# First layernorm of a transformer block: token-major rows and on-chip transposes replaced by embedding-major loads, with means and deviations applied separately

## The chip, the cores and the metric

The kernel runs on one core of a Trainium2 chip. The core has five instruction streams: TensorE (PE, matrix products, with its weight loads shown as PEld), VectorE (DVE), ScalarE (ACT), GpSimd (POOL) and SyncE (SP), which here issues every DMA. Each stream is executed in the order written, so an instruction that waits holds all behind it on its engine. The metric is the time of one execution in microseconds, median of several; all data are float32.

## The reference, cut to what matters

```python
def _layernorm(x, axis=-1, eps=1e-05):
    m = jnp.mean(x, axis=axis, keepdims=True)
    v = jnp.var(x, axis=axis, keepdims=True)
    return (x - m) / jnp.sqrt(v + eps)
...
    q = (hidden_states @ Wq).reshape(b, s, HEADS, HEAD_DIM)
    k = (hidden_states @ Wk).reshape(b, s, HEADS, HEAD_DIM)
    v = (hidden_states @ Wv).reshape(b, s, HEADS, HEAD_DIM)
    q, k = rotary(q), rotary(k)
    logits = jnp.where(causal, einsum('bhqd,bhkd->bhqk', q, k), MASK_VAL) / sqrt(64)
    out = einsum('bhqk,bhkd->bhqd', softmax(logits), v)
    return out.reshape(b, s, e) @ Wo
...
    x = x + _layernorm(attention(_layernorm(x)))
    x = x + _layernorm(ffn(_layernorm(x)))
```

There are 8 sequences (batches) of 512 tokens, an embedding of 1024, 16 heads of 64. The feed-forward part is one 1024x1024 product with a bias and a low-rank adapter. The change concerns the innermost layernorm, the one ahead of Wq, Wk and Wv. The mean and the deviation are one number per token, so (x - m)/d times a weight equals ((x - m) times the weight)/d. For q and k, d can therefore also be put into the cosine and sine tables of the rotary step, since these are multiplied onto every element of a token.

## The kernel before

All large products use two levels of Strassen-Winograd: 49 products of blocks in place of 64. The kernel goes through four stages: values (V = layernorm(x) @ Wv, batch after batch, and in passing the operands of x for later), q and k with attention, Wo, and the feed-forward part. The change touches the first stage, and the tables of the second.

**The V stage.** A loop over 8 batches, each of 7 groups of 7 products: 49 ticks (`N2`) a batch. In one tick PE does one 128x256 product over 256 rows (two calls, L315, four instructions in the trace). A group's products go into four accumulators: a and d with one buffer, b and c with two. The order in a group is P6 (accumulator b), P1 (a), P3 of the group before (c), P5 (c), P4 (d), P7 (b again), P2 (a again). They are drained one tick later (`Group.drain`, L334): P1 by a copy on ACT and the sum `u2 = p1 + b` on DVE, P7 by three sums on DVE, P2 by a copy on ACT, P3 by a sum on DVE. P7 accumulates onto the buffer that `u2` reads. Results are put together in tiles `c11`, `c21`, `c12`, `c22`, `U`, `A` (`COMBINE`, L358, some on DVE, some on POOL) and stored to `vd` by `store_v`.

**What is written by hand.** Nothing is planned by a scheduler: `at(tick, fn)` puts a function into a list, and `run` writes out, tick after tick, first what is marked "pe", then the tick's product with the drain of the one before, then the rest in order of registration. The order of instructions on each engine, SP too, is the order of these ticks.

**Operands of x.** While batch b is multiplied, `plan_x(b + 1, base)` (L468) prepares the next, with base = 49 b:
- ticks base-12 to base-9: four loads of 128 tokens x 1024 (`load_x`).
- ticks base+4 to base+23: mean and variance of each row (`stats`, L390: two `bn_stats`, an aggregate, a root on ACT, a reciprocal, a bias), and the norm on ACT in two halves (L415).
- ticks base+11, 18, 25, 32 and the ticks after each: four transposes each on PE (L449) and a copy on ACT into a tile of the right operand, `R11`, `R21`, `R12`, `R22` (L457).
- three ticks after the first transposes: the four differences of a tile on POOL (`sub_right`, L263).
- ticks 38, 45, 52, 63: the sums of tiles T1 (DVE), T2, T4 (POOL), T3 (DVE) (`sum_right`, L275). Tiles of one batch take the buffers of the batch before, by `next_roles`; T2 takes the buffer of the batch's T2, which product 44 is the last to read.
- each finished tile is also stored to `xop` for the second stage (`store_operand`, L463, 0.92 MB each).

**Weight sums.** In batches 1 to 7 the sums of one eighth of the q and k weights of the first half of the heads are made (`plan_part`, `plan_sums` L547, name `g0`): load at base (L553), eight operations on POOL at base+4 to base+11 (L562), store at base+16 (L565, 1568 KB in pieces of 256 bytes). The last batch does a second eighth on DVE.

**Second stage.** `plan_unit` (L691) forms q and k for two batches and half of the heads in a unit of 49 ticks, loads weights and operands of each tick 8 ticks ahead into a ring (`load_slot`, L606), and `rotate` (L660) multiplies by tables `cos` and `sin` (one of 128x512 each for all batches, loaded in `start_attention`). The attention of the unit before runs in between.

Of the kernel before, what the change touches and what calls it, by code (L numbers as in the profile page):

```python
# [132 lines left out]
def sandwich_kernel(  # L133
    ctx: ExitStack,
    tc: tile.TileContext,
    x: bass.AP,
    wqk: bass.AP,
# [31 lines left out]

    vd = [dram.tile([P, NT, E], F32, name=f"vd_{b}") for b in range(B)]  # L170
# [258 lines left out]
    xp = early.enter_context(tc.tile_pool(name="xp", bufs=4))  # L429
    chp = early.enter_context(tc.tile_pool(name="ch0", bufs=2))  # L430
    xs = {}
    dve, pool = nc.vector, nc.gpsimd

    def load_x(b, t):
        xs[b, t] = xp.tile([P, E], F32, tag="x", name=f"x_{b}_{t}")
        nc.sync.dma_start(out=xs[b, t], in_=x[b, ts(t, P), :])

    def stats_x(b, t, step):
        stats(f"v{b}_{t}", [xs[b, t][:, ts(h, HALF)] for h in range(2)], step)

    def norm_x(b, t):
        for h in range(2):
            v = xs[b, t][:, ts(h, HALF)]
            norm(f"v{b}_{t}", v, v)

    def transpose_x(b, t, g):
        pt = ps_t.tile([P, NH, P], F32, tag="tp", name=f"ptx_{b}_{t}_{g}")
        for k in range(NH):
            nc.tensor.transpose(pt[:, k, :], xs[b, t][:, ts(NH * g + k, P)], ident)  # L449
        return pt  # L450

    def keep_x(b, t, g, pt):
        h, c = divmod(t, 2)
        n = f"R{g + 1}{h + 1}"
        if c == 0:
            open_right(gvp, b - B, n)
        nc.scalar.copy(  # L457
            RX[b - B, n][:, 2 * c : 2 * c + 2], pt[:, :, :].rearrange("p (k c) n -> p k c n", k=2)
        )
# [4 lines left out]

    def store_v(b, tag, half, h):
        nc.sync.dma_start(out=vd[b][:, 2 * h : 2 * h + 2, ts(half, HALF)], in_=C[b - B, tag])

    def plan_x(b, base):  # L468

        at(base + 10, next_roles)  # L470
        for t in range(NT):
            at(max(0, base - 12) + t, lambda t=t: load_x(b, t))
            k = (4, 5, 17, 19)[t]
            for m in range(4):
                at(base + k + m, lambda t=t, m=m: stats_x(b, t, m))
            at(base + k + 4, lambda t=t: norm_x(b, t))
        for n, k in (("R11", 11), ("R21", 18), ("R12", 25), ("R22", 32)):
            g, h = int(n[1]) - 1, int(n[2]) - 1
            for c in range(2):
                t = 2 * h + c  # L480
                at(base + k + c, lambda t=t, g=g: transpose_x(b, t, g), "pe")
                at(base + k + c, lambda pt, t=t, g=g: keep_x(b, t, g, pt), "post")
            at(base + k + 3, lambda n=n: sub_right(b - B, n, pool))
# [7 lines left out]
        for n, k in (  # L491
            ("R11", 18), ("R21", 25), ("R22", 40), ("T1", 44), ("T2", 54), ("T4", 60), ("T3", 69)
        ):
            at(base + k, lambda n=n: store_operand(b, n))

    def prepare(t):
        for m in range(4):
            stats_x(0, t, m)
        norm_x(0, t)

    tags = {"L11": "L11", "L12": "L12", "L22": "L22", "L21": "S3"}
    nc.scalar.activation(eps_sd, eps, AF.Sqrt)
    for n in (0, 1, "L11", 2, 3, "L12", "L22", "L21"):
        if isinstance(n, int):
            load_x(0, n)
        else:
            load_left(wvp if n == "L21" else wvl, wv, n, tags[n])
    for t in range(2):
        prepare(t)
    for g in range(2):  # L510
        for t in range(2):
            keep_x(0, t, g, transpose_x(0, t, g))
    for k in range(4):
        sub_left("L11", k, dve)
# [3 lines left out]
    sub_right(-B, "R11", dve)  # L518
    at(0, lambda: sub_right(-B, "R21", dve))
    for t in (2, 3):  # L520
        at(t - 2, lambda t=t: prepare(t))
    for g in range(2):
        for t in (2, 3):
            at(3 + 2 * g + t - 2, lambda t=t, g=g: transpose_x(0, t, g), "pe")
# [836 lines left out]
```

## Time and profile before

| | us |
|---|---|
| runs before (3) | 2499.87, 2498.07, 2499.29; median 2499.29 |
| span of the profiled execution | 2491.9 |
| PE busy in the span | 2394.2 (96%) |
| DVE, POOL, ACT busy | 1744.9, 1490.5, 1094.4 |
| V stage: first product to first product of stage two | 13.0 to 431.8 |
| transposes L449 in it (x256), PE busy | 43.7 |
| bn_stats L395 (x64), norms L415 (x64) | 41.9, 48.6 |
| weight sums L562 on POOL to 420 us (x56) | 64.5 |
| DMA: q1 share of 16 engines over the span | 73.9% |

The span is 7.4 us shorter than the median of the runs, which also hold what lies before the first and after the last instruction. Rows of a timeline give the start, the length, the engine, the line, output and inputs, and in brackets the idle time of the engine before it and what ended that. Busy times of matmuls overlap, since they are pipelined; the distance between starts tells more. In names, a number such as -5 is the batch minus 8 (so -5 is batch 3), and the number after it only tells buffers apart.

### The profile page before, as it was taken

What the parts mean: (1) busy time and instruction counts of PE and PEld (TensorE: products, weight loads), DVE (VectorE), ACT (ScalarE), POOL (GpSimd) and SP (SyncE); (2) the same over time, 40 slices, a digit from 0 to 9 for tenths busy, and PEclk for the clock granted to TensorE, in tenths of its full rate; (3) what the DMA queues carried; (4) which work ended last, traced back from release to release, by engine and by line L of the source; (5) the groups of instructions that cost most, each with busy time, mean ns of one, the idle gap of its engine ahead of it and who ended that gap; (6) DMA issues with size and microseconds to landing.
All of it is one profiled execution on the core that took longest, in us unless ns stands there. A gap on an engine that the chain in (4) does not pass through costs nothing. (4 is left out here: it accounts for less than half of the span.)

```text
span 2491.9 us, 37087 instructions
## 1 busy us (share of the span) xinstructions
PE 2394.2 (96%) x12192; PEld 1880.4 (75%) x12192; DVE 1744.9 (70%) x3849; ACT 1094.4 (44%) x2749; POOL 1490.5 (60%) x1119
## 2 busy tenths in 40 slices
PE   6999999999999999999999999899999999999997
PEld 4787887877677777777777776458888878888886
DVE  8777767475857759486775957766777777766676
ACT  3323331026555556555555565763444544222222
POOL 3878875215263454637465363426777687888885
PEclk8999999999999999999999999899999999999999
DMA  7697787999899898988989895657566676434334
GB/s 261 198 299 251 241 272 235 344 307 285 238 302 285 258 328 255 328 267 297 326 264 346 250 327 174 219 182 266 178 202 212 217 278 240 137 126 153 132 106 140
DMA packets 415665, 606.00 MB, mean 243 GB/s; under 512 B 127889, under 2 KB 243601, under 8 KB 410866
## 3 DMA queue, kind: packets, MB, share of 16 engines
q1 hardware_dynamic: 415474, 603.64, 73.9%
q8 instruction: 98, 1.61, 0.3%
q14 instruction: 93, 0.76, 0.1%
HBM read 368.65 MB, written 201.33 MB: 229 GB/s over the span
## 5 line engine op out<-in xcount | busy, mean ns | idle before, releaser
L778 ACT ACTIVATE pr<-pr,nm 128x128 f32<-128x128 f32 (+3 forms) x512 | 280.9, 550 | 169.7 <-DVE nm L768 169.6
L792 ACT ACTIVATE pr<-pr,rs 128x128 f32<-128x128 f32 (+2 forms) x500 | 245.2, 549 | 119.9 <-DVE rs L786 119.8
L768 DVE CUSTOM_DVE_ANT_0 pr<-s,mask 128x128 f32<-128x128 f32 (+3 forms) x512 | 224.1, 484 | 41.8 <-PE s L747 39.7
L636 PE MATMUL acca_q_P<-xs,ls 128*128 128x256 f32 x896 | 217.3, 385 | 0.8 <-issue 0.8
L636 PE MATMUL accc_q_P<-xs,ls 128*128 128x256 f32 x896 | 217.7, 386 | 0.0
L636 PE MATMUL accb_q_P<-xs,ls 128*128 128x256 f32 x896 | 216.3, 384 | 0.8 <-DVE u_q_P L116 0.8
L1107 POOL TENSOR_TENSOR c<-c,row 128x512 f32<-128x512 f32 x120 | 160.7, 1360 | 87.4 <-ACT c L415 80.3
L636 PEld LDWEIGHTS acca_q_P<-xs,ls 128*128 128x128 f32 x896 | 165.3, 190 | 49.9 <-issue 19.1
L636 PEld LDWEIGHTS accc_q_P<-xs,ls 128*128 128x128 f32 x896 | 165.8, 190 | 48.4 <-issue 23.2
L636 PEld LDWEIGHTS accb_q_P<-xs,ls 128*128 128x128 f32 x896 | 165.4, 190 | 44.9 <-issue 6.2
L275 POOL TENSOR_TENSOR T<-R,T 128x512 f32<-128x512 f32 (+1 forms) x96 | 174.1, 1840 | 41.4 <-DVE u_P L337 21.0
L747 PE MATMUL s<-qk 64*128 64x128 f32 (+3 forms) x1024 | 193.8, 474 | 5.1 <-DVE nm L768 4.7
L806 PE MATMUL ptp<-ident,pr 128*128 128x128 f32 x1280 | 178.7, 278 | 11.0 <-DVE nm L768 4.8
L806 PEld LDWEIGHTS ptp<-ident,pr 128*128 128x128 f32 x1280 | 147.7, 142 | 43.1 <-ACT pr L792 15.8
L827 PE MATMUL po<-pT,v 128*64 128x512 f32 (+3 forms) x1024 | 157.4, 446 | 9.7 <-ACT pT L821 9.7
L562 POOL TENSOR_TENSOR wc_g<-wc_g 128x256 f32<-128x256 f32 (+1 forms) x120 | 124.1, 1053 | 65.5 <-DMA wc_g<-in_wqk_dram 43.5
L678 POOL TENSOR_TENSOR B_q<-B_q,m 128x1024 f32<-128x1024 f32 x14 | 35.0, 2497 | 199.0 <-DVE B_q L675 199.0
L827 PEld LDWEIGHTS po<-pT,v 128*64 128x64 f32 x1024 | 72.4, 139 | 102.0 <-issue 66.5
L337 DVE TENSOR_TENSOR p_P<-accb_P,p_P 128x256 f32<-128x256 f32 x109 | 45.0, 413 | 102.4 <-PE accb_P L315 53.5
L636 PE MATMUL accd_q_P<-xs,ls 128*128 128x256 f32 x448 | 108.7, 385 | 0.0
L337 DVE TENSOR_TENSOR u_P<-accb_P,p_P 128x256 f32<-128x256 f32 x109 | 46.1, 423 | 89.1 <-ACT p_P L342 89.0
L747 PEld LDWEIGHTS s<-qk 64*128 64x128 f32 x1024 | 73.1, 187 | 46.2 <-issue 27.9
(1108 smaller groups left out, 5809.7 us busy)
## 6 DMA issues: line engine op xcount, KB each, us to landing
ls<-wqk SPq DMA_DIRECT2D x392, 256.0 KB, 4.9
xs<-xop SPq DMA_DIRECT2D x392, 256.0 KB, 5.2
R<-attn SPq DMA_DIRECT2D x32, 896.0 KB, 5.5
wqk<-wc_g SPq DMA_DIRECT2D x16, 1568.0 KB, 9.3
x<-in_x_dram SPq DMA_DIRECT2D x32, 512.0 KB, 9.5
v<-vd SPq DMA_DIRECT2D x64, 256.0 KB, 5.0
attn<-ops SPq DMA_DIRECT2D x16, 1024.0 KB, 7.8
row<-in_x_dram SPq DMA_DIRECT2D x32, 512.0 KB, 5.9
```

The lines of the kernel that those rows point to most:

```text
L275: eng.tensor_tensor(RX[q, n][:, c], RX[q, x][:, c], RX[q, y][:, c], op=ALU.subtract)
L337: add = lambda out, x, a: nc.vector.tensor_tensor(out, acc[a], x, op=ALU.add)
L562: eng.tensor_tensor(out, x, y, op=op)
L636: nc.tensor.matmul(acc[:, :, w, :], lhsT=ls[:, k, w, :], rhs=xs_[:, :, k, :], start=(first and w == 0 and k == 0), stop=True, skip_group_c ...
L678: eng.tensor_tensor(v, v, m[step - 4, q], op=ALU.add)
L747: nc.tensor.matmul(ps[:, j, at : at + L], lhsT=qT[r, qb], rhs=kT[r, : qb + 1], start=True, stop=True,)
L768: nc.vector.tensor_tensor_reduce(out=v[:, j, :], in0=self.ps[qb][:, j, :], in1=work2["mask"][:, S - L :], scale=-1.0 / HD**0.5, scalar=3.0e38,
L778: nc.scalar.activation(v[:, j, :], v[:, j, :], AF.Exp, bias=nm[:, j : j + 1], scale=-1.0, accum_out=sm[:, j : j + 1],)
L792: nc.scalar.mul(v, v, rs[:, j : j + 1])
L806: nc.tensor.transpose(pt[:, n, :], self.pr[qb][:, j, ts(kb, P)], ident)
L827: nc.tensor.matmul(po[j * HD : (j + 1) * HD, kb * P :], lhsT=self.v[:, kb, ts(j, HD)], rhs=self.pT[j][:, kb, kb * P :], start=(kb == 0), s ...
L1107: nc.gpsimd.tensor_tensor(c, c, row[q, t][:, ts(h, HALF)], op=ALU.add)
```

## The change

The embedding-major form of x is a second input, `xt`, laid out on the host like the tiles `R11` to `R22`. Each tile is loaded straight into its operand buffer. The rows are still loaded, as one transfer of 2 MB a batch, only for sums and squared deviations, on ACT. The negative means go through a small DRAM tile `std` and come back spread over all partitions; `center` adds them to a loaded tile on DVE. For batch 0 the means are made on PE by products with a matrix of -1/1024. The operands are then centred but not divided. The inverse deviation goes onto the finished values (`scale_v`, ACT, ahead of each `store_v`) and, again by `std`, onto tables `tab0` and `tab1` of each unit of stage two (`load_inverse`, `scale_trig` on POOL), which `rotate` uses in place of `cos` and `sin`. The differences of the tiles move one tick or so later, and stores of tiles and values by up to three.

```diff
+    std = [dram.tile([2, S], F32, name=f"std_{b}") for b in range(B)]
...
-    xp = early.enter_context(tc.tile_pool(name="xp", bufs=4))
+    xp = early.enter_context(tc.tile_pool(name="xp", bufs=1))
+    mean_w = xp.tile([P, P], F32, name="mean_w")
+    nc.gpsimd.memset(mean_w, -1.0 / E)
...
+    def load_rows(b):
+        xs[b] = xp.tile([P, NT, E], F32, tag="x", name=f"x_{b}")
+        nc.sync.dma_start(out=xs[b], in_=x[b].rearrange("(t p) e -> p t e", p=P))
+        moments[b] = env["small"].tile([P, 4, NT], F32, tag="mom", name=f"mom_{b}")
+    def sum_rows(b, t):
+        m = moments[b]
+        nc.scalar.activation(xs[b][:, t], xs[b][:, t], AF.Copy, accum_out=m[:, 0, t : t + 1])
+    def square_rows(b, t):
+        m = moments[b]
+        nc.scalar.activation(
+            xs[b][:, t], xs[b][:, t], AF.Square, bias=m[:, 1, t : t + 1], scale=1.0,
+            accum_out=m[:, 2, t : t + 1],
+        )
...
+    def store_moment(b, w):
+        nc.sync.dma_start(
+            out=std[b][w].rearrange("(t p) -> p t", p=P), in_=moments[b][:, 1 + 2 * w]
+        )
+    def load_means(b):
+        means[b] = env["small"].tile([P, S], F32, tag="means", bufs=1, name=f"means_{b}")
+        nc.sync.dma_start(out=means[b], in_=std[b][0:1, :].to_broadcast([P, S]))
+    def load_xt(b, n):
+        open_right(gvp, b - B, n)
+        nc.sync.dma_start(
+            out=RX[b - B, n][:, 0:4].rearrange("p s c n -> p (s c n)"),
+            in_=xt[b, int(n[1]) - 1, int(n[2]) - 1],
+        )
+    def first_means(h):
+        pt = means[0, h] = ps_t.tile([P, 2, P], F32, tag="tp", name=f"pm_{h}")
+        for i in range(NK):
+            g, k, c = i // 4, i // 2 % 2, i % 2
+            nc.tensor.matmul(
+                pt, lhsT=mean_w, rhs=RX[-B, f"R{g + 1}{h + 1}"][:, k:4:2, c, :],
+                start=(i == 0), stop=(i == NK - 1),
+            )
+    def center(b, n):
+        h = int(n[2]) - 1
+        mean = means[0, h] if b == 0 else (
+            means[b][:, h * HT : (h + 1) * HT].rearrange("p (t n) -> p t n", t=2)
+        )
+        v = RX[b - B, n][:, 0:4].rearrange("p (t k) c n -> p t (k c) n", t=2)
+        nc.vector.tensor_tensor(
+            v, v, mean[:, :, :].unsqueeze(2).broadcast_to([P, 2, 4, P]), op=ALU.add
+        )
+    def scale_v(b, tag, h, j):
+        v = C[b - B, tag][:, j, :]
+        nc.scalar.mul(v, v, moments[b][:, 3, 2 * h + j : 2 * h + j + 1])
+    def plan_moments(b, k):
+        for t in range(NT):
+            at(k + t, lambda t=t: sum_rows(b, t))
+            at(k + 6 + t, lambda t=t: square_rows(b, t))
+        at(k + 5, lambda: neg_mean(b))
+        if b:
+            at(k + 6, lambda: store_moment(b, 0))
+            at(k + 10, lambda: load_means(b))
+        at(k + 11, lambda: root(b))
+        at(k + 12, lambda: inverse(b))
+        at(k + 13, lambda: store_moment(b, 1))
     def plan_x(b, base):
         at(base + 10, next_roles)
-        for t in range(NT):
-            at(max(0, base - 12) + t, lambda t=t: load_x(b, t))
-            k = (4, 5, 17, 19)[t]
-            for m in range(4):
-                at(base + k + m, lambda t=t, m=m: stats_x(b, t, m))
-            at(base + k + 4, lambda t=t: norm_x(b, t))
+        at(max(0, base - 12), lambda: load_rows(b))
+        plan_moments(b, base - 5 if b > 1 else 3)
         for n, k in (("R11", 11), ("R21", 18), ("R12", 25), ("R22", 32)):
-            g, h = int(n[1]) - 1, int(n[2]) - 1
-            for c in range(2):
-                t = 2 * h + c
-                at(base + k + c, lambda t=t, g=g: transpose_x(b, t, g), "pe")
-                at(base + k + c, lambda pt, t=t, g=g: keep_x(b, t, g, pt), "post")
-            at(base + k + 3, lambda n=n: sub_right(b - B, n, pool))
+            at(base + k - 1, lambda n=n: load_xt(b, n))
+            at(base + k + 3, lambda n=n: center(b, n))
+            at(base + k + 4, lambda n=n: sub_right(b - B, n, pool))
...
-            ("R11", 18), ("R21", 25), ("R22", 40), ("T1", 44), ("T2", 54), ("T4", 60), ("T3", 69)
+            ("R11", 20), ("R21", 26), ("R22", 41), ("T1", 44), ("T2", 54), ("T4", 60), ("T3", 69)
...
+    at(2, lambda: first_means(1), "pe")
     for k, n in ((5, "R12"), (7, "R22")):
+        at(k - 1, lambda n=n: center(0, n))
         at(k, lambda n=n: sub_right(-B, n, dve))
...
+    at(18, lambda: load_rows(0))
+    plan_moments(0, 27)
...
-        for k, tag, half, h in ((22, "c11", 0, 0), (53, "c21", 1, 0), (54, "c12", 1, 1), (57, "c22", 0, 1)):
+        for k, tag, half, h in ((23, "c11", 0, 0), (56, "c21", 1, 0), (52, "c12", 1, 1), (58, "c22", 0, 1)):
+            if b == 0 and k == 23:
+                k = 45
+            for j in range(2):
+                at(base + k - 2 + j, lambda b=b, tag=tag, h=h, j=j: scale_v(b, tag, h, j))
             at(base + k, lambda b=b, tag=tag, half=half, h=h: store_v(b, tag, half, h))
...
+    def load_inverse(u, s):
+        t = inv[u] = trig.tile([P, NT, P], F32, tag="inv", name=f"inv_{u}_{s}")
+        src = std[2 * (u % (B // 2)) + s][1:2, :].to_broadcast([P, S])
+        nc.sync.dma_start(out=t[:, :, :].rearrange("p t n -> p (t n)"), in_=src)
+    def scale_trig(u, s, i):
+        if not s:
+            tabs[i] = trig.tile([P, NT, 2, P], F32, tag=f"tab{i}", name=f"tab{i}_{u}")
+        t = (cos, sin)[i].rearrange("p (t n) -> p t n", t=NT)
+        nc.gpsimd.tensor_tensor(tabs[i][:, :, s], inv[u], t, op=ALU.mult)
     def plan_unit(u, base):
+        for s in range(2):
+            at(base + 10 + 10 * s, lambda s=s: load_inverse(u, s))
+            for i in range(2):
+                at(base + 16 + 10 * s + i, lambda s=s, i=i: scale_trig(u, s, i))
...
+    at(2, lambda: nc.sync.dma_start(out=cos, in_=rope[0]))
+    at(2, lambda: nc.sync.dma_start(out=sin, in_=rope[1]))
```

## The prediction

> **What bounds the kernel now.** I read the page first, then windows by stage, then the timeline of one batch.
>
> ```profile
> PE 2394.2 (96%) x12192; PEld 1880.4 (75%) x12192; DVE 1744.9 (70%) x3849; ACT 1094.4 (44%) x2749; POOL 1490.5 (60%) x1119
> ...
> PEclk8999999999999999999999999899999999999999
> ```
>
> TensorE is busy 96% of the span at nearly full clock, so a gain must shorten its stream. The windows (length, then PE, PEld, DVE, ACT, POOL busy, granted clock, DMA share, GB/s) say where that is possible:
>
> ```profile
> 150.00:200.00 50.00, 48.17 (x234) 40.66 (x233) 36.14 (x69) 16.41 (x35) 39.86 (x36) 1.00 0.80 262
> 425.00:450.00 25.00, 23.81 (x110) 20.35 (x109) 11.77 (x16) 2.50 (x5) 4.46 (x2) 1.00 1.03 380
> ...
> 18.00:20.00 2.00, 0.00 (x0) 0.00 (x0) 2.00 (x4) 0.00 (x0) 2.00 (x2) 1.00 0.93 340
> 20.00:22.00 2.00, 0.00 (x0) 0.00 (x0) 1.57 (x6) 0.57 (x2) 1.92 (x3) 0.63 1.10 399
> 22.00:24.00 2.00, 1.41 (x6) 1.33 (x7) 1.46 (x5) 1.52 (x4) 2.00 (x2) 0.50 0.53 216
> 24.00:26.00 2.00, 2.00 (x8) 1.61 (x7) 0.26 (x1) 2.00 (x4) 1.92 (x3) 0.50 0.00 0
> 206.00:208.00 2.00, 1.96 (x10) 1.38 (x8) 1.91 (x5) 0.54 (x2) 1.92 (x3) 1.00 0.87 218
> 216.00:218.00 2.00, 2.00 (x13) 1.75 (x12) 0.85 (x2) 0.21 (x2) 0.34 (x1) 1.00 1.03 339
> ```
>
> In the V stage (150 to 200) PE is busy 48.17 of 50, beside POOL at 39.86 and DVE at 36.14; the attention stage (425 to 450 is its start) has long windows at 25.00 of 25. The rows at 18 to 26 show the clock: after 7 us without a matmul it stands at 0.50. The last two are the DMA rate inside the store of weight sums (218 GB/s) and after it (339).
>
> The timeline of PE in batch 2 (start, length):
>
> ```profile
> 167.34 1.03 PE L315 MATMUL accc_-6_P<-wv_L,R_-6_917 128*128 128x256 f32 x4
> 168.20 0.60 PE L449 MATMUL ptx<-ident,x 128*128 128x128 f32 x4
> 168.64 1.03 PE L315 MATMUL accd_-6_P<-wv_L,R_-6_917 128*128 128x256 f32 x4
> ...
> 170.80 1.03 PE L315 MATMUL acca_-6_P<-wv_L,R_-6_917 128*128 128x256 f32 x4
> ```
>
> A product (tick) takes 0.865 us, a group of four transposes 168.64-168.20 = 0.44. A batch is 49 products and 8 groups: 42.4+3.5 = 45.9 us; batches start 49.0 apart ((380.20-86.23)/6), so some 3 us are waits. POOL in the same batch:
>
> ```profile
> 180.55 6.23 POOL L275 TENSOR_TENSOR T_-5_1414<-R_-5_1333,T_-5_1372 128x512 f32<-128x512 f32 x3 [3.82 <-DVE u_-6_P L337]
> 186.74 4.47 POOL L355 TENSOR_TENSOR c_-6_1236<-c_-6_1236,U_-6_1393 128x512 f32<-128x512 f32 x2
> 191.17 4.27 POOL L275 TENSOR_TENSOR T_-5_1453<-R_-5_1217,T_-5_1414 128x512 f32<-128x512 f32 x3
> 195.40 9.20 POOL L562 TENSOR_TENSOR wc_g<-wc_g 128x256 f32<-128x256 f32 x8
> ```
>
> T2 can start only when product 44 has released its buffer (T2 at 180.55, product 45 at 180.30; in two other batches the releaser named is PE's accc, not DVE). Then POOL runs without a pause: T2 6.2, c21 4.5, T4 4.2, eight weight sums 9.2, to 204.6. What SP then issues, how long that store takes to land (minimum, median, maximum), and what SP waits for (total, times, longest):
>
> ```profile
> 204.62 0.56 SPq L565 DMA_DIRECT2D wqk<-wc_g  x1
> 208.57 3.44 SPq L463 DMA_DIRECT2D xop<-R_-4_1532  x1
> ...
> 216.25 5.00 SPq L436 DMA_DIRECT2D x<-in_x_dram  x3
> ```
>
> ```profile
> DMA to landing us min/median/max: 9.1/9.1/9.3
> ```
>
> ```profile
> SPq L565 <- POOL wc_g L562: 69.5, 12, 9.6
> ```
>
> The store of weight sums, asked for at tick 16 of a batch, goes out 24.1 us after T2 began, about tick 19, because SP waits for POOL. Today only stores and loads with 12 or more ticks of lead stand behind it.
>
> **The change part by part.** The sum is against the profiled execution, span 2491.9; the median of the three runs, 2499.3, is 7.4 above it, and I add differences to the median.
>
> *Transposes out.* 256 leave PE. In batches 0 to 6 that is up to 7x3.5 = 24.5 us, and the waits on them (4.4 us on norms in 86 to 380, 0.75 a batch behind ACT's square root) go too. Alone, a batch would take 42.4 plus about 1.5: 44, or 5 less for each of batches 1 to 6.
>
> *DVE.* Out: 64 bn_stats (41.9 us), aggregates, reciprocals, biases (6.7+4.8+6.8): 60. In: 32 centres of 128x1024, from 1.2 us (the combine at 427.73, POOL quiet) to 2.17 (182.93, beside POOL): 38 to 70. Even; DVE has 28% free.
>
> *ACT.* Out: 64 norms (48.6), 32 roots (9.3), 64 copies at 0.59 (37.5). In: 64 passes over 128x1024, between 1.03 (copies of 256 and 512 at 0.37 and 0.59, extended) and 1.6 (twice a norm of 0.807); I take 1.4, as these too go SBUF to SBUF: 90; and 64 scalings of v at 0.807: 52. Net +47 on an engine at a third. But in ticks 44 to 60 it gets eight passes, six scalings and the drains, 11.2+4.8+1.5 = 17.5 us in 16x0.865 = 13.8, and the scaling of c21 (tick 54) waits for POOL's c21 at T2+10.7, tick 57. The drains of accumulator a behind it are late: PE stops 2 to 5 us a batch there. That costs nothing where a later stop absorbs it (next).
>
> *SP, the step that decides.* Operands were made on chip; now each is a 0.52 MB load at ticks 10, 17, 24, 31, its centre on DVE four ticks (3.5 us) later. R21's load (17) is queued behind the store of weight sums (16), which waits for POOL. From T2's start: store issued at 24.1, plus 0.5 because the centre of R11 now contends with POOL (bounds 0 and 1.0: T2 took 6.2 beside two such DVE operations, T4 of the same size 4.2; I take the middle, since the eight sums already run beside some DVE work), so 24.6; landed +9.2 = 33.8. The load is behind it on the same queue, which the next operand store also shows (R-5_1162, issued 4.0 after its weight store at 155.5, lands 7.9 later, 11.9 in all: 9.2 plus its 0.92 MB at 340 GB/s). So +1.5: R21 lands at 35.3. DVE, in order, has stood at the centre since tick 21; behind it is queued the u2 sum that reads accumulator b, and PE's product 26 accumulates there. PE reaches it at 30x0.865 = 26.0 plus its stops, and goes on at 35.3+1.2+0.4+0.2 = 37.1: idle for up to 11 us, minus ACT's 2 to 5. Then 19 products to the next T2, 16.4 us, plus 2.5 for half clock (0.50 to 0.66 for some 5 us after the idle from 16 to 22): 56.0 a batch against 49.0.
>
> R12's load (24) follows 2.9 MB behind R21 and lands at 35.3+8.5 = 43.8; the centre adds 1.2+0.4 to 45.4, and PE needs it at product 33, 37.1+6.1+2.5 = 45.7: just free. R22 lands at about 48, needed at 52. POOL ends R22 and c21 at 55: free, by 1 us. Ends for a batch: 51 (POOL as in quiet rows of the attention stage, 7.5 for the eight sums, so store at 22.4; landing 9.1; no clock loss) to 58 (R12 and R22 late by 1 each).
>
> The Trainium skill, TensorE: Matmul & The Clock Gate, Part 1, gives about 3.4 us busy before full clock returns, after an idle window as long; that would make the clock loss an estimated 1.7 instead of 2.5, 5 us less over six batches, and it speaks against a change that opens such gaps. SBUF — State Buffer, two separate sides, lets a DVE operation with two SBUF inputs block POOL fully, and bn_stats has one input: its estimate is a whole centre, 1.2 us on POOL's chain instead of my 0.5, 4 us more in all. No row here shows a centre, so I keep the rows' values.
>
> *Moments, means.* 15 stores of 512 four-byte elements, means (0.26 MB) asked for 9 ticks ahead: bounds 0 and 2 us a batch, near 0, as they lie before T2+24. SP's load of means waits until the store of moments has landed; behind it stand two stores and R11's load, whose centre comes before the weight sums end. The scaling of the mean (tick 49) makes DVE wait for ACT's sums, with the drains behind it: part of the 2 to 5 us above. In batch 1's preparation the means are asked for one tick ahead: 5 us on a DVE-bound batch 0.
>
> *Start and batch 0.* First product near 14.8 (13.0 before): 8 mean products, centre, differences. Batch 0 is DVE-bound, saves four statistics (1.9 each) and pays three centres and the wait for means; first T2 at 78 to 92, I take 84 against 86.4.
>
> *Attention.* POOL scales 4 tables a unit, 32x1.27 (opt rows) = 41 us, where it is half idle; 16 loads of 0.26 MB. PE is full there: 0; ring loads have 8 products (13.8 us) of lead; if that cover went, 5 us a unit.
>
> Sum: six loops from T2 to T2 took 376.99-86.43 = 290.6; now 6x56.0 = 336.0; first T2 -2.4: +43. Batch 7 has no operand load: unchanged. 2499.3+43 = 2542.
>
> **Rivals.**
> 1. Faster: R21 isn't late. Break-even is its landing at T2+30.2 (48.4, the mean of the six loops, -16.4-1.8, no clock loss). For: loads of v land 5.0 after issue; with POOL quiet (store at 22.4) and the load served beside the store it lands at 22.9+5.0 = 27.9: 46.1 a batch, 2499-14-2 = 2483; with PE as the only bound, 44 a batch, 2499-27-2 = 2470. Against: the operand store above, and POOL's 24.1 repeats.
> 2. Slower still: R12 and R22 stop PE too. At the 285 GB/s of a mixed slice R12 lands 1.6 later, half clock comes twice (2.5): 60 a batch, 2499+69-2 = 2566. For: 1 us of slack. Against: DMA after the store ran at 339.
> 3. POOL's tables hold SP and with it the ring: 8 units x 3 = 24 us on top of the forecast, 2563. Against: lead of 13.8.
> 4. The two effects balance: landing at 30 to 31, 49 a batch, 2500.
>
> **How the numbers follow.** Forecast 0.66, its own range 6x51 to 6x58 with the first T2 at 78 to 92: 2506 to 2562. Rival 1 0.14, 2 and 3 together 0.15, 4 0.05. Leaving out rival 1 (0.14) and some 0.05 at the far end of 2 and 3: 2486 to 2574. A measurement tells 0.2% (5 us) from no change: faster 0.14, same 0.05, slower 0.81.
>
> **What would show it.** Right: the weight store still 23 to 25 us after T2, R21's load next on SP, DVE idle on that load for 8 us or more, then PE idle at the fifth accumulation of the group, clock 0.5 after it, batches 54 to 58 apart; the attention stage as long as before. Wrong if DVE's idle time before the centres is under 3 us a batch, or ACT's passes, not R21, end PE's waits.

## The result, and the profile after

The changed kernel took 2649.9 us (median of four runs, 2642.4 to 2652.2) against 2499.6 for the kernel before: 1.059 times as long, 95% interval 1.057 to 1.062. The forecast of slower was right, the size was not: 2542 was predicted, at most 2574. The profiled execution has a span of 2650.3 against 2491.9, 158.4 more. The trace divides this as follows.

| stage | before | after | difference | predicted |
|---|---|---|---|---|
| first product | 13.0 | 12.8 | -0.3 | +1.8 |
| start of T2 in batch 0 | 86.4 | 103.1 | +17 | -2.4 |
| six loops from T2 to T2 | 6 x 48.4 | 6 x 68.7 | +122 | +45 |
| first product of q and k | 431.8 | 571.0 | +139 | |
| attention stage and Wo, to the first adapter product | 1306.5 | 1326.5 | +20 | 0 |
| the rest | 753.6 | 752.9 | -1 | 0 |

The last row but one is called the attention stage below; Wo has 126 us of it in both kernels.

The page's first line and its row of granted clocks answer to those shown of before:

```profile
PE 2412.8 (91%) x11968; PEld 1883.6 (71%) x11968; DVE 1740.5 (66%) x3737; ACT 1117.0 (42%) x2789; POOL 1537.4 (58%) x1152
...
PEclk8888888899999999999999999999999999999999
```

TensorE was 96% busy and is 91%; the first eight slices, nearly all of the V stage, now have a clock of 0.8. What happens there is read from one batch. SP's issues after T2 at 237.79 (start, length of the issue):

```profile
246.31 0.36 SPq L469 DMA_DIRECT2D std<-mom  x1
...
257.13 0.33 SPq L477 DMA_DIRECT2D means<-std  x1
...
258.03 0.49 SPq L469 DMA_DIRECT2D std<-mom  x1
...
259.47 0.56 SPq L481 DMA_DIRECT2D R_-4_1227<-in_xt_dram  x1
...
260.74 2.86 SPq L617 DMA_DIRECT2D wqk<-wc_g  x1
263.69 18.13 SPq L481 DMA_DIRECT2D R_-4_1269<-in_xt_dram  x1
```

The first store of moments goes out at 246.31, and the load of means, which reads it back, only at 257.13, since SP stands until the store has landed. Then the second store of moments goes out ahead of R11's load. The store of weight sums follows at 260.74, 23 us after T2 and 0.5 us after POOL's last sum (260.22). The issue of R21's load behind it takes SP 18 us; the trace names no wait for that, and a full queue is the likely reason.

How long a store of moments takes to land (minimum, median, maximum), and what SP waits for at the load of means (total, times, longest):

```profile
DMA to landing us min/median/max: 9.8/12.9/16.2
```

```profile
SPq L477 <- DMA std<-mom: 61.0, 7, 11.0
```

A store of 2 KB takes 9.8 to 16.2 us, more than the 1568 KB of weight sums took before (9.1). The windows show why. The columns are the stretch, its length, then PE, PEld, DVE, ACT and POOL busy, granted clock, DMA share, GB/s. A DMA packet's whole time counts in the window in which it starts, so a share can be over 1:

```profile
250.00:252.00 2.00, 1.25 (x6) 0.76 (x4) 0.96 (x3) 2.00 (x5) 2.00 (x2) 1.00 2.25 93
252.00:254.00 2.00, 0.44 (x2) 0.42 (x3) 0.18 (x1) 2.00 (x5) 1.92 (x3) 1.00 1.01 19
...
266.00:268.00 2.00, 0.00 (x0) 0.00 (x0) 0.00 (x0) 0.00 (x0) 0.00 (x0) 1.00 1.39 45
268.00:270.00 2.00, 0.00 (x0) 0.00 (x0) 0.00 (x0) 0.00 (x0) 0.00 (x0) 0.59 1.17 32
...
274.00:276.00 2.00, 0.00 (x0) 0.00 (x0) 0.02 (x1) 0.00 (x0) 0.00 (x0) 0.50 1.04 369
```

The DMA engines count as busy all the time, at 19 to 93 GB/s from 250 to 254 and at 32 to 45 from 266 to 270, where the first and the second store of moments lie in the queue; behind the second, R11's load runs at 369. So R11's centre can start only 16.5 us after the issue of its load. What DVE and then TensorE wait for in that batch (total, times, longest):

```profile
DVE R_-4_1227 L502 <- DMA R_-4_1227<-in_xt_dram: 14.3, 1, 14.3
```

```profile
PE accb_-5_P L317 <- DVE u_-5_P L339: 18.6, 4, 13.2
```

DVE stands 14.3 us at R11's centre, and TensorE 13.2 at the accumulation that waits for the DVE sum queued behind it; the clock is at 0.50 before it goes on. The same pair of waits stands in all six loops (12.8 to 15.8 us at R11, 12.5 to 15.4 on TensorE).

### The profile page after: what moved, and what is told of

Same layout as the page of the kernel before. It is cut to its first block, busy times and chain, and to the rows that moved or that the text cites. A ratio compares the mean times of both kernels' runs of the same rounds, so it can differ in the third digit from the quotient of the medians.

```text
span 2650.3 us, 36633 instructions
## 1 busy us (share of the span) xinstructions
PE 2412.8 (91%) x11968; PEld 1883.6 (71%) x11968; DVE 1740.5 (66%) x3737; ACT 1117.0 (42%) x2789; POOL 1537.4 (58%) x1152
## 5 line engine op out<-in xcount | busy, mean ns | idle before, releaser
L688 PEld LDWEIGHTS acca_q_P<-xs,ls 128*128 128x128 f32 x896 | 166.4, 191 | 50.5 <-issue 19.2
L688 PEld LDWEIGHTS accc_q_P<-xs,ls 128*128 128x128 f32 x896 | 165.8, 190 | 48.9 <-issue 20.6
L877 PE MATMUL ptp<-ident,pr 128*128 128x128 f32 x1280 | 179.3, 278 | 18.9 <-ACT pr L863 10.4
L898 PE MATMUL po<-pT,v 128*64 128x384 f32 (+3 forms) x1024 | 159.6, 446 | 12.2 <-ACT pT L892 11.1
L614 POOL TENSOR_TENSOR wc_g<-wc_g 128x256 f32<-128x256 f32 (+1 forms) x120 | 114.2, 970 | 70.1 <-DMA wc_g<-in_wqk_dram 44.8
L339 DVE TENSOR_TENSOR p_P<-accb_P,p_P 128x256 f32<-128x256 f32 x109 | 45.0, 413 | 102.4 <-PE accb_P L317 53.4
L265 POOL TENSOR_TENSOR R<-R 128x256 f32<-128x256 f32 x128 | 97.8, 774 | 17.7 <-DMA R<-x1t 11.2
```

Of the source, the lines that this page charges most:

```text
L265: eng.tensor_tensor(t[:, out], t[:, x], t[:, y], op=ALU.subtract)
L614: eng.tensor_tensor(out, x, y, op=op)
L688: nc.tensor.matmul(acc[:, :, w, :], lhsT=ls[:, k, w, :], rhs=xs_[:, :, k, :], start=(first and w == 0 and k == 0), stop=True, skip_group_c ...
L877: nc.tensor.transpose(pt[:, n, :], self.pr[qb][:, j, ts(kb, P)], ident)
L898: nc.tensor.matmul(po[j * HD : (j + 1) * HD, kb * P :], lhsT=self.v[:, kb, ts(j, HD)], rhs=self.pT[j][:, kb, kb * P :], start=(kb == 0), s ...
```

## The experiments

Theory S: the 512 pieces of 4 bytes in each store of moments hold the load queue for some 8 us, and two of them stand ahead of R11's load. The rivals: Q, the step that the prediction put first (a load with a lead of four ticks behind the weight-sum store); W, SP's standing still until the first store has landed. Batch lengths below are the mean of six, from T2 to T2.

**Moments stored in rows.**

```diff
+        nc.tensor.transpose(pt[:NT, 0, :], moments[b][:, 1 + 2 * w], ident)
...
+        nc.vector.tensor_copy(rows[b, w], pt[:NT, 0, :])
...
-            out=std[b][w].rearrange("(t p) -> p t", p=P), in_=moments[b][:, 1 + 2 * w]
+        nc.sync.dma_start(out=std[b][w].rearrange("(t p) -> t p", p=P), in_=rows[b, w])
```

> Edit: TensorE turns the 128x4 tile of moments into 4 rows before each of the 15 stores, so that a store is 4 runs of 512 bytes instead of 512 pieces of 4 bytes. Nothing else moves; the weight-sum store is still just ahead of R21's load. Theory S (the small pieces hold the load queue, some 8 us for each store, two stores a batch ahead of R11's load): the stores land in 2 to 4 us, R11 lands under 8 us after issue, the stop at R11 goes, and the mechanism of the prediction (R21 behind the weight-sum store) comes up from under it: batches 54 to 58 apart instead of 68.7, 2570 in all (2555 to 2590). Theory Q (what holds PE is only the short lead of four ticks and the queue's order, not the size of the pieces): batches stay at 66 to 70, 2640 or more.

Measured: 2554.3 us, 1.023 (1.019 to 1.026), batches 55.9 apart, first T2 at 89.0. The shape of 15 stores of 2 KB is worth 96 of the 150 us, 92 of them by the end of the V stage (479.1 against 571.0). The stores still take 5.2 to 8.5 us to land, not the 2 to 4 that were expected, but R11's centre starts 4.9 to 5.9 us after the issue of its load, where it was 13.6 to 16.5. And under it lies what the prediction described. SP's issues after T2 at 201.64:

```profile
212.72 0.27 SPq L477 DMA_DIRECT2D std<-row  x1
...
218.10 0.27 SPq L477 DMA_DIRECT2D std<-row  x1
219.50 0.35 SPq L487 DMA_DIRECT2D R_-4_1263<-in_xt_dram  x1
...
224.12 0.56 SPq L625 DMA_DIRECT2D wqk<-wc_g  x1
226.07 6.01 SPq L487 DMA_DIRECT2D R_-4_1305<-in_xt_dram  x1
```

DVE's centres of R11 and R21 in the same batch, with what they waited for:

```profile
224.97 1.23 DVE L508 TENSOR_TENSOR R_-4_1263<-R_-4_1263,means 128x1024 f32<-128x1024 f32 x1 [0.32 <-DMA R_-4_1263<-in_xt_dram]
...
236.91 1.23 DVE L508 TENSOR_TENSOR R_-4_1305<-R_-4_1305,means 128x1024 f32<-128x1024 f32 x1 [5.92 <-DMA R_-4_1305<-in_xt_dram]
```

The weight-sum store goes out 22.5 us after T2 (predicted 24.6), R21's load directly behind it, and R21's centre starts at T2+35.3 (predicted landing 35.3). R11 is no longer late. TensorE's two stops in this batch, by windows:

```profile
205.00:209.00 4.00, 2.83 (x13) 1.84 (x12) 3.89 (x5) 0.76 (x2) 4.00 (x3) 1.00 0.68 189
209.00:213.00 4.00, 3.05 (x14) 2.42 (x15) 2.47 (x5) 4.00 (x7) 4.00 (x3) 1.00 0.25 96
213.00:217.00 4.00, 1.69 (x9) 1.16 (x8) 0.96 (x4) 4.00 (x10) 4.00 (x4) 1.00 0.86 275
217.00:221.00 4.00, 4.00 (x13) 3.08 (x12) 1.04 (x3) 0.76 (x2) 3.77 (x6) 0.57 1.04 320
...
233.00:237.00 4.00, 0.81 (x4) 0.38 (x2) 0.10 (x1) 0.00 (x0) 0.00 (x0) 1.00 0.96 285
237.00:241.00 4.00, 2.48 (x6) 2.03 (x7) 2.17 (x4) 0.00 (x0) 2.58 (x4) 0.56 1.08 384
241.00:245.00 4.00, 4.00 (x13) 3.21 (x12) 1.47 (x4) 0.37 (x1) 0.28 (x1) 0.59 1.05 370
```

```profile
238.52 2.07 PE L317 MATMUL accb_-5_P<-wv_S,T_-5_1116 128*128 128x256 f32 x4 [4.71 <-DVE u_-5_P L339]
```

It idles 3.2+1.5 = 4.7 us at R21, and before that 4.4 us from 205 to 217: 1.2 at the transpose of the means, which only this experiment has, 0.9 at a `u2` sum and 2.3 at ACT's copy of A. ACT has its passes, its scalings and the drains there (4.00 of 4.00 busy from 209 on).

**The second store alone, out of the way.**

```diff
-        at(k + 13, lambda: store_moment(b, 1))
+        at(k + (13 if b == 0 else 41), lambda: store_moment(b, 1))
```

> Edit: the store of inverse deviations (the second of the two stores of small pieces a batch) is asked for 28 ticks later, behind all four operand loads. Theory S (each such store holds the queue for some 8 us): R11's load loses one of the two holds ahead of it; batches 59 to 63 apart instead of 68.7, 2605 in all (2585 to 2625). Theory W (what costs is SP standing at the load of means until the first store has landed, 10 us a batch, and not the queue): batches stay 67 to 70 apart, 2640 or more.

Measured: 2603.7, 1.042 (1.039 to 1.046), batches 61.6 apart: 7.1 us less a batch, the price of one such store ahead of R11, whose centre starts 7.0 to 8.1 us after the issue of its load. SP's wait at the load of means is still there (first store at 231.65, means at 242.51 in the batch after T2 at 220.73).

**No waiting for the first store.**

```diff
-        nc.sync.dma_start(out=means[b], in_=std[b][0:1, :].to_broadcast([P, S]))
+        nc.sync.dma_start(out=means[b], in_=std[b - (b > 1)][0:1, :].to_broadcast([P, S]))
```

> Edit: from batch 2 on the load of means reads the row that the batch before stored, so SP has nothing to wait for there; the same stores and loads go out in the same order (the output is computed with another batch's means). Theory W (SP's wait for the landing of the first store is what delays R11): R11's load goes out 8 us or more sooner, batches 57 to 61 apart, 2595 in all (2575 to 2610). Theory S (the two holds of the queue remain ahead of R11, and SP's wait only adds what it does not share with them): batches 63 to 68 apart, 2630 in all (2612 to 2650).

Measured: 2635.6, 1.055 (1.052 to 1.058), batches 66.9 apart. SP no longer stands at the load of means, but R11's load goes out only 1 to 2 us sooner in five of the six loops (4 in the first), not the 8 of theory W, and DVE still waits 11.1 to 13.6 us at its centre: the pieces are ahead of it all the same. W is worth 14 us of 150; S holds.

**The stores on another queue.**

```diff
-        nc.sync.dma_start(
+        nc.scalar.dma_start(
```

> Edit: the 15 stores of moments are issued by ACT to its own queue instead of by SP. Theory S with the order of one queue as the reason: R11's load no longer stands behind the pieces and lands under 10 us after issue; batches 54 to 60 apart, 2575 in all (2555 to 2600). Theory S with the DMA engines themselves as the reason (all queues share them): while a store goes through, the others' rate falls as before, R11 still lands 12 us or more after issue, batches 64 to 70 apart, 2635 in all (2615 to 2660).

Measured: 2632.8, 1.054 (1.051 to 1.057), batches 66.0 apart. ACT issues the second store of one batch at 241.07, R11's load goes out on SP's queue at 246.93, and is centred at 260.69. The windows between:

```profile
249.00:251.00 2.00, 2.00 (x11) 1.77 (x10) 0.59 (x1) 0.37 (x1) 0.04 (x1) 1.00 1.24 77
251.00:253.00 2.00, 1.49 (x7) 0.96 (x6) 0.00 (x0) 0.00 (x0) 0.00 (x0) 1.00 0.76 53
...
255.00:257.00 2.00, 0.00 (x0) 0.00 (x0) 0.00 (x0) 0.00 (x0) 0.00 (x0) 0.50 0.85 103
257.00:259.00 2.00, 0.00 (x0) 0.00 (x0) 0.00 (x0) 0.00 (x0) 0.00 (x0) 0.50 1.02 382
```

With the pieces on another queue the rate of all transfers still falls to 53 GB/s, and rises to 382 when they are through. So it is the DMA engines that are held, not the order of one queue. The Trainium skill, DMA: Bandwidth & Descriptors, Issuing engines are not separate DMA queues, says that transfers end on the same 16 engines whoever starts them, and that a second issuing engine saves issue time alone; this run agrees, with 17 of 150 us saved.

**The same pieces in the kernel before.**

```diff
+        at(base + 1, lambda: store_zero(b, 0))
+        at(base + 8, lambda: store_zero(b, 1))
```

(store_zero stores a tile of zeros in the same shape.)

> Edit, on the kernel before: 14 stores of 512 pieces of 4 bytes (zeros, to a place that nobody reads), at ticks 1 and 8 of batches 0 to 6, where the changed kernel has its own. Theory S (each store holds the queue and the DMA engines for about 8 us; the loss in the changed kernel comes from what stands behind it with a lead of four ticks): the hold shows here too, a rate under 100 GB/s for 5 us or more at each store, but what stands behind it here has 12 ticks or more of lead, so the time grows by 0 to 25 us, 2497 to 2522. Theory X (pieces so small delay everything on the chip, whatever its lead): 14x8 = 112 us more, 2600.

Measured: 2515.2, 1.008 (1.005 to 1.011). The 14 stores land 14.6 to 21.0 us after issue and hold the engines here too (the first window is ahead of one store, the second inside it):

```profile
207.00:210.00 3.00, 3.00 (x18) 2.64 (x17) 2.96 (x5) 0.47 (x2) 2.92 (x3) 1.00 1.07 393
...
213.00:216.00 3.00, 3.00 (x15) 2.38 (x14) 2.80 (x9) 1.11 (x3) 3.00 (x3) 1.00 1.15 71
```

But they cost 20 us in all, 1.5 each, against 7.1 each in the changed kernel. The loads of x behind them have a lead of 12 ticks here, and no engine waits for one. What is late is an operand store behind the pieces: ACT waits for the buffer that it reads, once in each of six batches, 1.7 to 5.3 us and 18.4 in all, and in the kernel before never. The longest of these waits is in the same batch:

```profile
224.11 1.07 ACT L460 COPY R_-4_1675<-ptx 128x512 f32<-128x512 f32 x2 [5.25 <-DMA xop<-T_-5_1470]
```

The hold is that of the pieces; its price goes with what stands behind it and how soon that is needed. That the lead alone makes the difference is not shown, since the two kernels differ in more.

**The weight-sum store behind the loads** (with moments in rows).

```diff
-            plan_part(chp, "g0", n, (base, 1, base + 16))
+            plan_part(chp, "g0", n, (base, 1, base + 33))
```

> Edit: the kernel with moments stored in rows of 512 bytes, and besides the store of weight sums moved from tick 16 to tick 33 of a batch, behind the four operand loads. In that kernel without this second part the batches are 55.9 apart, R21's load is issued 1.95 us behind the weight-sum store and its centre starts 35.3 us after T2. Theory Q (the step of the prediction: R21's load stands behind that store): DVE's idle time before R21's centre goes, R21 is centred 28 to 31 us after T2, and the batches fall to 47 to 50: 2554 less 6x7 = 2512 (2498 to 2525). Theory B (the load is late through the transfers themselves, four loads and their stores in a row, and the place of the weight-sum store does not matter): batches stay 54 to 57, 2540 or more.

Measured: 2544.5, 1.020 (1.017 to 1.023), batches 53.4 apart: neither theory's batches, though the total is in theory B's. R21 is now centred without a wait in all six loops, where DVE stood 4.3 to 6.0 us with rows alone, so the store was the cause of that wait; but in the batch after T2 at 301.97 the centre starts only at T2+33.5 (28 to 31 expected), and the gain is 2.5 us a batch instead of 6 to 9. DVE waits up to 3.2 us for R11 now, and 3.2 to 5.5 for R12 (2.4 to 3.5 before). ACT's wait for the rows of x, in 90 to 575, shows what came besides:

```profile
ACT x L446 <- DMA x<-in_x_dram: 24.8, 5, 6.7
```

The 2.1 MB of rows (tick 37) now stand behind the store, ACT at its first sum for up to 6.7 us, and TensorE's drains behind ACT.

**Rows of x 14 ticks earlier and their sums 15, centres three later** (on top of the last).

```diff
-        at(max(0, base - 12), lambda: load_rows(b))
...
+        at(max(0, base - (26 if b > 2 else 12)), lambda: load_rows(b))
...
-            at(base + k + 3, lambda n=n: center(b, n))
...
+            at(base + k + 6, lambda n=n: center(b, n))
```

> Edit: on top of rows and late weight sums, the rows of x and their sums from batch 3 on are taken 14 and 15 ticks earlier (out of the ticks in which ACT scales v), and every centre comes 6 ticks after its load's place instead of 3, with the operand stores behind them. If TensorE is then the only bound, as the faster rival of the prediction has it, the batches from 2 on are 43.5 to 46 apart and the whole is 2478 to 2505, where the attention stage keeps its 20 us more. If ACT's passes, or POOL's differences that now come later and meet T2, hold PE: 47 to 50 apart, 2505 to 2530.

Measured: 2534.5, 1.016 (1.013 to 1.019), batches 53.0 apart: a miss. The rows land no better among the operand loads; ACT waits 4.9 us for them in the batch from 303 to 356, and a drain behind it holds DVE 6.4.

**The rows of x ahead of the weight-sum store** (with moments in rows).

```diff
-            plan_part(chp, "g0", n, (base, 1, base + 16))
+            plan_part(chp, "g0", n, (base, 1, base + (38 if n < B - 2 else 33)))
...
-        at(max(0, base - 12), lambda: load_rows(b))
+        at(max(0, base - (17 if b > 2 else 12)), lambda: load_rows(b))
```

> Edit: moments stored in rows, the weight sums stored at tick 38 (behind the four operand loads), and from batch 3 on the 2.1 MB of rows of x loaded at tick 32 instead of 37, ahead of that store. With the weight sums stored at tick 33 and the rows still at 37 the batches were 53.4 apart, 2.5 better than with the store at 16, and ACT stood up to 5.9 us at its first sum until the rows had landed, with a drain of TensorE's accumulator queued behind it. Theory H (the store of weight sums was only moved from in front of R21's load to in front of the rows' load, and took its 5 us with it): the wait for rows goes, batches 47 to 50.5 apart, 2510 in all (2495 to 2528). Theory L (the queue as a whole is too full for leads of a few ticks, whatever the order): some other load becomes the late one, batches 52 to 55, 2535 or more.

Measured: 2526.2, 1.011 (1.009 to 1.014), batches 51.1 apart, just past the end of theory H's 47 to 50.5. ACT's wait for rows is gone; TensorE now loses 4.4 us a batch in the ticks in which ACT has passes, scalings and drains together (1.2 of it at the transpose of the means). The next one, on top of this, gave nothing more:

```diff
-        plan_moments(b, base - 5 if b > 1 else 3)
+        plan_moments(b, base - (8 if b > 2 else 5) if b > 1 else 3)
...
+            at(base + 12, lambda s=s: load_inverse(u, s))
+            for i in (1, 0):
+                at(base + 15, lambda s=s, i=i: scale_trig(u, s, i))
```

> Edit, on top of the last one: the sums over the rows of x start 3 ticks earlier and the turning of the moments 3 ticks later against them, each centre comes 6 ticks after its load's place instead of 3, with the operand stores behind it; and in the attention stage the inverse deviations are loaded straight into the table of cosines, and all four scalings of a unit stand together at tick 15, in the stretch in which POOL has nothing to do (83 us of waiting ahead of its B additions in all units). If the leads and POOL's place were what was left to fix: batches 45 to 48 apart, the attention stage 1306 to 1313 long instead of 1319 to 1326, 2478 to 2505 in all: about the kernel before. If DVE and ACT's own work holds the batch (their drains stand behind centres and sums wherever these are put): batches 50 to 53, 2510 to 2530.

Measured: 2530.8, 1.013 (1.012 to 1.015), batches 52.4 apart, attention stage 1319.4. TensorE now waits 4.1 to 4.7 us for ACT's copy of A in each of five batches (2.4 at most before this edit): ACT's passes, three ticks earlier, stand in front of that drain. A miss in both halves.

**ACT's squares out of the ticks with the scalings; then the leads** (on top of the rows of x ahead).

```diff
+        late = 12 if b > 1 else 0
...
-            at(k + 6 + t, lambda t=t: square_rows(b, t))
+            at(k + 6 + late + t * (4 if late else 1), lambda t=t: square_rows(b, t))
...
-        nc.gpsimd.tensor_tensor(tabs[i][:, :, s], inv[u], t, op=ALU.mult)
+        nc.vector.tensor_tensor(tabs[i][:, :, s], inv[u], t, op=ALU.mult)
```

> Edit, on the kernel with rows of moments, late weight sums and the rows of x at tick 32 (batches 51.1 apart, 2526): from batch 2 on ACT's four squares of a batch, and the root, the inverse and their store behind them, are taken out of the ticks in which ACT also scales v, to ticks 13 to 25 of the next batch, where ACT has little to do; and the rotary tables are scaled by DVE instead of POOL. Theory A (what is left of the V stage's loss is ACT's pile of passes and scalings, in which TensorE stops 4.4 us a batch in the windows from 249 to 261): batches 46 to 48.5 apart, 15 to 30 us less. For the tables: if they cost through POOL (its F sums come late for DVE's rotations), the attention stage falls from 1318.6 to 1306 to 1313; if DVE is as tight as POOL, it stays 1316 to 1326. Both together 2485 to 2510. Theory D (DVE's centres and drains hold the batch, ACT only seems to): batches stay 50 to 52, 2512 to 2526.

Measured: 2523.4, 1.011 (1.006 to 1.016), batches 50.4 apart, attention 1319.5: theory D's numbers, but not its reason. TensorE's stop beside ACT went, and another took its place, at R11's centre, where DVE waited 3.4 to 5 us for the load. So the lead is next:

```diff
-            at(base + k + 3, lambda n=n: center(b, n))
-            at(base + k + 4, lambda n=n: sub_right(b - B, n, pool))
+            at(base + k + 6, lambda n=n: center(b, n))
+            at(base + k + 7, lambda n=n: sub_right(b - B, n, pool))
```

> Edit, on the kernel with late squares (batches 50.4 apart, 2523): every centre comes 6 ticks after its load's place instead of 3, its differences on POOL and the operand stores behind it, and TensorE turns the moments one and two ticks later from batch 2 on. Theory L (what is left is the lead: DVE still stands 3 to 5 us a batch at R11's centre for a load that shares the queue with four stores, and TensorE stops 3 to 4 us behind it at half clock after): that stop goes, batches 45 to 47.5 apart, 2493 to 2508. Theory D (DVE and POOL are full around T2, and differences that come later meet them): batches 49 to 52, 2512 to 2532. In both the attention stage stays near 1319.

Measured: 2509.8, 1.006 (1.004 to 1.008), batches 48.9 apart; the total misses theory L's 2508 by 2 us and the batches by 1.4, theory D's 2512 and 49 by 2 and 0.1: between the two. DVE's waits for operand loads in the V stage are down to 6.3 us in all, from 136.8 in the changed kernel. One batch before, and one here (windows from T2 to T2):

```profile
180.55:229.66 49.11, 47.27 (x230) 39.87 (x229) 35.25 (x67) 16.04 (x34) 39.06 (x34) 1.00 0.80 261
```

```profile
182.97:230.99 48.02, 43.76 (x200) 36.90 (x199) 36.89 (x55) 19.07 (x40) 40.60 (x34) 1.00 0.99 315
```

The transposes are gone from TensorE (43.76 busy instead of 47.27), and it still idles 4.3 us where it idled 1.8, with the DMA engines at 0.99 instead of 0.80. The change does take 3.5 us off TensorE's stream, and the batch is as long as before: the waits name two of DVE's drains in each of the six (2.0 to 2.9 us and 1.5), and DVE is busy for 36.9 us of a batch instead of 35.3. This was the best version of the changed kernel, and it does not beat the kernel before. Of what is left, most is not in the V stage: that ends at 435.8 us here and at 431.8 before, while the attention stage takes 1319.8 against 1306.5.

**The attention stage.** Three runs on the changed kernel alone leave out work of seven units, which keep the first unit's tables or its row of deviations: scalings and loads, scalings only, loads only.

```diff
-        for s in range(2):
+        for s in () if u else range(2):
```

> Edit, on the changed kernel alone: the rotary tables are scaled in the first unit only and kept for the other seven, so 28 of 32 scalings on POOL (28x1.27 = 36 us) and 14 of 16 loads of inverse deviations are left out (the output is computed with the first pair's inverse deviations). Theory P (the attention stage grew by 20 us because of this work): the stage from the first product of q and k to the first adapter product returns from 1326 to 1306 to 1312, 2632 in all (2622 to 2640). Theory N (it grew for another reason, the new shape of the rotations or the loads of cos and sin): it stays 1320 or more, 2645 or more in all.

> Edit, on the changed kernel alone: the rotary tables are scaled in the first unit only, and all 16 loads of inverse deviations (0.26 MB each, on SP's queue between the operands of the products) stay. The attention stage took 1306.5 before, 1326.5 after, and 1309.5 with scalings and loads both taken out of seven units. Theory P (the scalings: 5 us a unit of POOL's time, behind which DVE's rotations and then ACT's scalings come late): the stage stays at 1309 to 1313. Theory M (the loads: traffic on a queue whose operands have 8 products of lead): it is 1318 to 1327.

> Edit, on the changed kernel alone: the inverse deviations are loaded once, for the first table, and all 32 scalings on POOL go on with that one row (the output is computed with one batch's inverse deviations). Theory P (the scalings on POOL): the attention stage is 1318 to 1327. Theory M (the loads): 1309 to 1313.

Measured: the stage took 1309.5 without both (2642.0 in all), 1316.0 with the loads only (2629.3) and 1313.2 with the scalings only (2625.5). In all, the last two came out lower than the first because their V stages ended at 558 and 564 instead of 572; only the stage's own length says anything here. Without both, the stage came as theory P of that run said (1306 to 1312), though the total did not; of the two halves, the loads came out between the theories and the scalings at the end of theory M's 1313. So this work makes the stage longer: the eight kernels that have it unchanged lie between 1318.6 and 1326.5, which is 9 to 17 more than without it. The halves, 6.5 and 3.7 more from one profile each, lie inside the spread of 8 us of those eight kernels, so how the cost divides between loads and scalings, or whether it lies in their overlap, stays open. What the trace of the changed kernel shows of the way it takes:

```profile
DVE m L724 <- POOL F_q L706: 12.2, 5, 4.5
...
PE ptp L877 <- ACT pr L863: 10.4, 14, 1.9
```

POOL's sums of F come late by the scalings, DVE stands at the rotation (3.5 us before), ACT scales softmax rows later, and TensorE's transposes wait 10.4 us for them (4.0 before). This chain was read, not isolated; moving the scalings on POOL, or to DVE, changed nothing (1319.4, 1319.5), so the way stays open.

## Why the prediction was right or wrong

*Moments, means* is the step that failed: "15 stores of 512 four-byte elements" with "bounds 0 and 2 us a batch, near 0". A store costs 7.1 us a batch, and two stand ahead of R11's load: 12.8 us a batch in all, and 14 of the 17 us by which the first T2 is late (taken at 84, measured 103.1, and 89.0 with rows; in batch 0 DVE stood 12.9 for the means, where 5 were predicted; with rows it was 3.8). I counted bytes where pieces had to be counted, and took the place before T2+24 as cover, though R11's load stands right behind it. The trace of before has no store with such pieces, so the price of a piece was open, and the upper bound should have been the landing of the nearest store (9.1), not 2.

*SP, the step that decides* was right in its mechanism and its times, but masked: with the pieces gone, store, load and centre came as written, the batches were 55.9 apart where 56.0 were forecast, and the total, 2554.3, lies in the forecast's range. That close a hit is partly luck. TensorE goes on behind R21 at T2+36.9 (37.1 forecast), but it idles 4.7 us there, not the 6 to 9 that the step gives after *ACT*'s part, since it had come later: it had stood 4.4 us before, 3.3 of them behind ACT, and lost time to the clock. That R21's stop takes in ACT's was therefore right. DVE's idle time at R21 was 4.3 to 6.0 us, not the 8 or more that was named as a sign. TensorE's busy time is 47.3 us a batch there and 43.8 where the clock stays at 1.00, so the two stops cost 3.6 us of clock, where 2.5 was taken for one. In the windows above, a full window of 4 us has 20 matmul records; after the first stop 7 of them are missing, and from TensorE's start behind R21 some 13. That divides the 3.6 into about 1.3 and 2.3, an estimate. So 2.5 was about right for R21, and the estimate of 1.7 from the Trainium skill, TensorE: Matmul & The Clock Gate, Part 1, fits the first stop better than R21's. What the prediction set against the page on SBUF, a centre that holds POOL up, was not put to the test: in the batch shown of the kernel with rows the weight sums were over (store issued at 224.12) when R11's centre began (224.97).

*Transposes out* holds: 47.27-43.76 = 3.5 us a batch, as forecast.

*DVE* and *ACT*: a centre took 1.2 us as a rule (1.2 to 3.0, 1.2 to 2.2 forecast), a pass 1.04 to 1.15 and 0.19 for its sum (1.4 taken), a scaling of v 0.72 (0.807 taken). The sizes were right or a little high, but for the longest centre.

*Attention* was costed at 0, or 5 us a unit if the ring's cover went; it was 20 in all, 2.5 a unit. That cover held, since TensorE does not wait for a ring load in that stage; which other way the 20 us take, the runs do not settle, and the prediction did not look at the chain through POOL, DVE and ACT.

*Rivals*: R21 not late never came true as it stood, and the versions in which it was made true did not get near 44 us a batch: the best has 48.9, since ACT's passes, the rows of x and the leads each take the next place. The sum of rival 3, 24 us on top of 2542, is 2566 and not 2563. The test "R21's load next on SP, DVE idle on that load for 8 us or more" would have told the wrong load: it was R11.

## What to carry to other kernels

Count the pieces of a store, not its bytes: turn a column of scalars into rows on the chip before it is stored. Before an operand's production is replaced by a load, list what stands ahead of that load on the DMA engines, at whatever queue, and compare it with the lead. And when one transfer is moved out of the way of another, ask at once which load now stands behind it.

## What the runs showed of the hardware that was not expected

A store of 512 pieces of 4 bytes holds the DMA engines for about 7 us (7.1 by the time that one less saves a batch). Shared evenly by 16 engines that is some 0.22 us a piece, an estimate worked out as 7.1/32. The trace's packet records do not show this time at the pieces: those of the store issued at 246.31 stand between 247.2 and 247.6, 8 ns each. It shows at the packets behind them: of 2 KB each, they took 0.09 us until 250 and then up to 6.6 us, until 257.5. What the engines wait for in that time is not shown. With the stores on ACT's queue the rate of all transfers falls too, to 53 GB/s at the lowest.

The clock does not answer to a stop's length alone. In the kernel with rows and in the one with early rows, TensorE makes the same stop of 2.31 us for the same drain, behind two that are equal as well (1.16 and 0.95 us in the one, 1.16 and 0.94 in the other; the timeline of TensorE; start, length, and the idle time before it in brackets):

```profile
216.20 1.34 PE L317 MATMUL acca_-5_P<-wv_L,R_-5_1001 128*128 128x256 f32 x4 [2.31 <-ACT A_-5_1227 L351]
```

```profile
260.28 1.13 PE L317 MATMUL acca_-4_P<-wv_L,R_-4_1304 128*128 128x256 f32 x4 [2.31 <-ACT A_-4_1531 L351]
```

After the first, the window from 217 to 221 above has a clock of 0.57; after the second, the clock stays at 1.00:

```profile
257.00:261.00 4.00, 1.69 (x8) 1.19 (x7) 1.04 (x4) 4.00 (x10) 4.00 (x4) 1.00 0.87 289
261.00:265.00 4.00, 4.00 (x20) 3.43 (x20) 1.13 (x3) 0.82 (x2) 3.77 (x6) 1.00 0.90 303
```

The Trainium skill, TensorE: Matmul & The Clock Gate, Part 1, has the clock judged over a window that runs freely, whatever the kernel does. That two equal stops end differently agrees with it.
